# Patch sets of the second block in tiles of their own, and lookups, scatters and weight preparation at other places, in a two-layer codebook convolution

## The chip, the cores and the metric

The kernel runs on one core of one Trainium2 chip. The metric is the device time of one execution in microseconds (us), as the median of several executions. A core has TensorE (PE, matrix products), VectorE (DVE), ScalarE (ACT), GpSimd (POOL) and SyncE (SP), which here only issues transfers; the transfers themselves are moved by 16 DMA engines.

## The reference

The input x is 16 images of 256 channels of 28 x 28. It is normalised in groups of 8 channels, goes through two layers of an approximate 3 x 3 convolution, each with a batch normalisation, and through a squeeze-and-excite gate; the result is added to the normalised and to the raw input.

```python
def amm_conv3x3(x, centroids, w_sub, stride=1):
    patches = jax.lax.conv_general_dilated_patches(x, (3, 3), (stride, stride), 'SAME')
    p = patches.reshape(B, C, s, Ho * Wo).transpose(0, 3, 1, 2)
    d = jnp.sum(p * p, axis=-1)[..., None] - 2.0 * jnp.einsum('bncs,cks->bnck', p, centroids) + jnp.sum(centroids * centroids, axis=-1)[None, None]
    attn = jax.nn.softmax(-d, axis=-1)
    lut = jnp.einsum('cks,cso->cko', centroids, w_sub)
    out = jnp.einsum('bnck,cko->bno', attn, lut)

out = amm_conv3x3(x, centroids1, wsub1, stride=1)
out = jax.nn.relu(bn_inference(out, ...))
out = amm_conv3x3(out, centroids2, wsub2, stride=1)
out = se_layer(bn_inference(out, ...), se_w1, se_b1, se_w2, se_b2)
return jax.nn.relu(out + x)        # x is the group-normalised input; the caller adds the raw one
```

For each channel a patch of 9 values is compared with 16 centroids, and the softmax over them weights the rows of a product of centroids and weights.

## The kernel before

**Blocks and steps.** The work of an image in a layer is cut into four blocks: a half of the channels (`hh`) by a half of the rows (`t`), in the order (0,0), (0,1), (1,1), (1,0). There are 128 blocks, layer 1 first. A block starts every two steps: block j has g = 2j, an image takes 8 steps, layer 2 starts at step 128. The order of all work is written out by hand: `at(step, sub, f, ...)` (L896) files a job under a step and a place within it, and L1111 calls them sorted by that pair. Each call appends its instructions to the queues of the engines it uses, and every engine works through its own queue in that order; an instruction that waits holds up what stands behind it on its engine. TensorE's logits lie at sub 0.1 and 1.1, block sums and numerators (`num_b`, `num_a`) at 1.0, products with the weights at 2.0.

**A block.** `patches(u, p)` (L368) issues six transfers on SyncE that gather the 3 x 3 patches of 64 channels from a padded copy in DRAM (`home1` for layer 1, `home2` for layer 2) into a tile of 128 x 8 x 420. A block has two such sets, p = 0 and 1. There are two tiles, `pts[0]` and `pts[1]`, which all blocks share, so set p of a block is issued at step g + p - 2, after the logits of the block before have read the tile. One row in 16 of the tile stays 1.0 (a bias row); it is filled once at the start, `pts[0]` by ScalarE (L1098) and `pts[1]` by POOL (L1102). `logits` (L380) makes 32 small matmuls for each of four quarters `mm`, ScalarE takes exponentials (`exps`), `num_b` sums the weights, VectorE makes the reciprocal (`recip_dve`) and spreads it over the partitions (`spread`), and `scale_a` (VectorE), or `copy_a` and `scale_q` (ScalarE, POOL) scale the numerators.

**Products.** The four blocks of an image are combined with seven weight tiles of 128 x 9 x 128: A11, A12, A22 and S1 to S4, sums and differences of the weights (a Strassen-like scheme, `PRODUCTS`, L43). POOL makes differences of the activations (`mix`, L527). In layer 1 A11, S3, A22 and A12 are loaded (`load_w`, L194) and S1, S3, S2, S4 are made from them in steps 5 to 8 (`combine`, L207); layer 2 loads all seven near step 128.

**The start.** x of image 0 is loaded in two halves of channels; each is normalised (`norm0`: VectorE, TensorE, POOL, ScalarE) and written to `home1` (`to_home1`, L362). Block 0 and block 1 use the first half of the channels, block 2 and block 3 the second. `center_wd` prepares the centroids (`center_sq` on VectorE, a matmul in `center_add`, then `center_mean`: a reduction, a small multiply and a subtraction, L294). `load_x(1)`, the statistics of image 1 (`gn_stats`) and the loads of A11, S3, A22, A12 follow at steps 1 to 6.

**Preparation during layer 1.** Layer 2 uses its channels in a sorted order that depends on image 0's output. `rank_look` (L664) looks up tables with two indirect transfers of POOL, `rank_cols` copies seven columns for each half; `to_home2` (L593) scatters an image's output with indirect transfers of POOL. Image 0's output is kept in DRAM and read again by `h0_load` and scattered by `h0_put`. The second layer's centroids and weights are laid out in a staging tile `st`: `prep_wd0` to `prep_wd4` centre them in steps 57 to 78 (`prep_wd4`, L739: the mean by VectorE, two subtractions on POOL), `prep_cwa` (L756) makes four multiplies on VectorE and a transfer in step 82, `prep_cwb` (L764) six small POOL operations a part in steps 83, 84, 91 and 92.

The places that matter before:

```python
at(g + p - NPT, 1.5, patches, u, p)                          # L927, NPT = 2
at(*((g - 2, 2.6) if b else (1, 1.65)), load_x, b + 1)        # L1000
at(18, 2.15, rank_look, o)                                    # L1044
at(78, 1.9, prep_wd4)                                         # L1064
at(82, 1.9, prep_cwa)                                         # L1067
at(-0.5, 0.7, to_home1, 0, 1)                                 # L1106
```

Of the kernel before, what the change touches and what calls it, by code (L numbers as in the profile page):

```python
# [8 lines left out]
F32 = mybir.dt.float32  # L9
I32 = mybir.dt.int32  # L10
U32 = mybir.dt.uint32
AF = mybir.ActivationFunctionType
ALU = mybir.AluOpType
# [63 lines left out]
def kernel(  # L77
# [113 lines left out]

    wl = {n: wpool.tile([P, NS, P], F32, name=f"w_{n}") for n in SLOTS}

# [48 lines left out]

    pts = [const.tile([P, 8, PTW], F32, name=f"pt{i}") for i in range(NPT)]
    hpads = [io.tile([P, NPAD], F32, tag="pc", name="hpad", bufs=4) for _ in range(NB)]
    xpads = [io.tile([P, NPAD], F32, tag="pc", name="xpad", bufs=4) for _ in range(NB)]
# [47 lines left out]

    def center_mean(wf, n, eng=None):  # L294
        g = wf.rearrange("p (g k) -> p g k", k=K)
        nc.vector.tensor_reduce(cst[:, : n // K], g, axis=AX.X, op=ALU.add)
        nc.vector.tensor_scalar_mul(cst[:, : n // K], cst[:, : n // K], 1.0 / K)
        (eng or nc.vector).tensor_sub(g, g, cst[:, : n // K].unsqueeze(2).to_broadcast([P, n // K, K]))

# [436 lines left out]
    def prep_wd3(part, step):  # L736
        center_add(pw["st"][:, 512:1536], 384 * part, min(384, 1024 - 384 * part), pw["sq"], step)

    def prep_wd4():  # L739
        st = pw["st"]  # L740
        center_mean(st[:, 512:1536], 1024, nc.gpsimd)
        f = st[:, 512:1536].rearrange("p (g n) -> p g n", n=32)
        nc.gpsimd.tensor_sub(f, f, kbias.unsqueeze(1).to_broadcast([P, 32, 32]))
# [152 lines left out]
    def at(cl, sub, f, *a, **kw):  # L896
        jobs.setdefault((cl, sub), []).append((f, a, kw))
# [23 lines left out]
    for j, u in enumerate(blocks):  # L921
# [3 lines left out]
        for p in range(2):  # L925
            u["pt", p] = pts[p]
            at(g + p - NPT, 1.5, patches, u, p)  # L927
            for q in range(2):
                mm = 2 * p + q
                at(g + p, 0.1 + q, logits, u, mm)  # L930
                if wide and mm == 0:
                    at(g, 0.12, wide_copy, u, mm)
                    at(g, 0.9, wide_turn, u, mm)
                    at(g, 1.38, wide_max, u, mm)
                    at(g, 1.39, wide_sub, u, mm)
                    at(g + 1, 1.22, wide_back, u, mm)
                    at(g + 1, 1.89, wide_exp, u, mm)
                else:
                    at(g + p, 0.12 + q, exps, u, mm)
# [18 lines left out]
    for l in range(2):  # L958
        for b in range(B):
# [30 lines left out]
            if l == 0:  # L990
# [8 lines left out]
                if b + 1 < B:  # L999
                    at(*((g - 2, 2.6) if b else (1, 1.65)), load_x, b + 1)  # L1000
                    for q in range(NB):
# [26 lines left out]

    at(1, 1.66, load_w, 0, "A11")
    at(3, 1.65, load_w, 0, "S3")  # L1030
# [10 lines left out]
    for o in range(2):  # L1041
        at(14, 2.95, rank_make, o)
        at(16, 0.2, rank_sum, o)
        at(18, 2.15, rank_look, o)  # L1044
    for o in range(2):
        at(19 + o, 2.7, rank_cols, o)
        at(24 + 2 * o, 0.6 + 2 * o, h0_load, o)
        for r in range(2):
            at(25 + 2 * o + r, 0.2 if r else 1.9, h0_put, o, r)
        at(32 + 2 * o, 2.6, codes_load, o)  # L1050
# [9 lines left out]
    for part in range(3):  # L1060
        c = (68, 70, 76)[part]
        at(c, 1.95, prep_wd2, part)
        at(c + 1, 2.1, prep_wd3, part, c + 1)
    at(78, 1.9, prep_wd4)  # L1064
    at(78, 2.7, prep_keep, d_wd[1])
    at(80, 2.6, prep_cw0)
    at(82, 1.9, prep_cwa)  # L1067
    for part in range(4):
        at((83, 84, 91, 92)[part], (2.3, 1.5, 2.3, 1.5)[part], prep_cwb, part)
    at(92, 2.7, prep_keep, d_cwb)  # L1070
# [29 lines left out]
    for i in range(2):  # L1100
        to_home1(0, 0, i)
    nc.gpsimd.memset(pts[1], 1.0)  # L1102
    center_wd(0)
    norm0(1)
# [167 lines left out]
```

## Time and profile before

| | us |
|---|---|
| median of 3 runs | 2643.18 (2643.03 to 2647.02) |
| the profiled execution | 2635.26 |
| its span | 2633.8 |
| VectorE busy in it | 1757.6 |
| ScalarE busy | 1357.3 |
| POOL busy | 1898.4 |

The profile is one execution as the hardware profiler saw it, in us from the start of its span. In a timeline row stand the start, the length, the engine, the line of the kernel, the operation, what it writes and reads, the size, and a count where several were merged; in brackets the time for which the engine was idle before it and what ended that. PEld is TensorE's loading of weights, SPq the issue of transfers by SyncE. The chain of waits follows the work that ended last back through what released each piece.

### The profile page before, as it was taken

The page shows a single profiled execution, that of the slowest core. Times are in us where ns is not written, and L with a number is a line of the kernel's source. Part 1 is how long each engine was busy: PE and PEld are TensorE (multiplying, and loading weights), DVE is VectorE, ACT ScalarE, POOL GpSimd, SP SyncE. Part 2 cuts the span into 40 slices and gives each one's busy share as a digit, 9 for nine tenths or more (in the row PEclk, how much of TensorE's full clock was granted, in tenths as well). Part 3 has the DMA queues.
Part 4 walks back from the last instruction along what each step waited for, and adds up shares of the span by engine and source line. Part 5 has one row for each costly group of instructions (what it writes and reads, how often), then busy time and mean ns, then how long its engine had stood idle before and what let it go on. Part 6 is the DMA issues. An engine that isn't in the chain of part 4 may idle for free.

```text
span 2633.8 us, 85661 instructions
## 1 busy us (share of the span) xinstructions
PE 2582.8 (98%) x36984; PEld 1262.6 (48%) x36984; DVE 1757.6 (67%) x3760; ACT 1357.3 (52%) x1874; POOL 1898.4 (72%) x1318
## 2 busy tenths in 40 slices
PE   5999999999999999999999999999999999999997
PEld 2444454444544444544444444444444444444444
DVE  4776566666566665656666776767776667767665
ACT  4444444445444444444455555555555655555653
POOL 2866667766667766687667778778878787777786
PEclk8999999999999999999999999999999999999999
DMA  7656655665455666655664444444444444444441
GB/s 206 163 156 178 192 157 162 189 182 165 141 149 145 173 179 170 174 154 157 163 174 103 115 115 118 129 114 114 106 128 127 117 119 112 116 118 126 114 121 46
DMA packets 217831, 374.37 MB, mean 142 GB/s; under 512 B 29752, under 2 KB 188008, under 8 KB 217448
## 3 DMA queue, kind: packets, MB, share of 16 engines
q1 hardware_dynamic: 211272, 336.16, 48.1%
q0 software_dynamic: 6176, 32.66, 3.4%
q8 instruction: 295, 4.83, 0.8%
q14 instruction: 88, 0.72, 0.1%
HBM read 288.93 MB, written 79.80 MB: 140 GB/s over the span
## 4 chain that ended last, share of the span: by engine, by line
PE 96%; DVE 2%; POOL 1%; DMA 0%; issue 0%; SPq 0%; ACT 0%; DVEq 0%; POOLq 0%; ACTq 0%
PE acc L522 52%; PE lg L388 17%; PE nb L452 14%; PE na L438 13%; DVE rb L495 0%; POOL qp L531 0%; DMA pt<-home 0%; DVE r L480 0%; DVE qp L514 0%; SPq L375 0%; PE sep L820 0%; PE sqp L291 0%; POOL qp L503 0%; PE sep L809 0%; DMA xt<-in_x 0%
## 5 line engine op out<-in xcount | busy, mean ns | idle before, releaser
L399 ACT ACTIVATE e<-lg 128x784 f32<-128x784 f32 x960 | 738.0, 821 | 654.7 <-PE lg L388 652.0
L531 POOL TENSOR_TENSOR qp<-qp,qp 128x784 f32<-128x784 f32 x512 | 943.9, 1868 | 155.1 <-DVE qp L514 154.6
L522 PE MATMUL acc<-qp,w_S 128*128 128x392 f32 x2048 | 733.1, 501 | 2.0 <-POOL qp L531 1.1
L495 DVE STREAM_SHUFFLE rb<-r 128x392 f32<-128x392 f32 x1024 | 550.7, 603 | 0.0
L522 PE MATMUL acc<-qp,w_A 128*128 128x392 f32 x1536 | 546.5, 499 | 0.0
L522 PEld LDWEIGHTS acc<-qp,w_S 128*128 128x128 f32 x2048 | 375.6, 190 | 345.2 <-issue 52.5
L388 PE MATMUL lg<-pt,wd 32*32 32x392 f32 x16384 | 485.4, 502 | 19.8 <-DMA pt<-home 11.1
L522 PEld LDWEIGHTS acc<-qp,w_A 128*128 128x128 f32 x1536 | 284.1, 190 | 247.6 <-DVE qp L514 40.2
L466 DVE SCALAR_TENSOR_TENSOR r<-nb,kst,r 128x392 f32<-128x392 f32 x128 | 79.9, 624 | 467.9 <-ACT r L462 448.3
L452 PE MATMUL nb<-e,cwb 64*32 64x392 f32 x8192 | 375.5, 494 | 0.1
L438 PE MATMUL na<-e,cwa 64*32 64x392 f32 x8192 | 374.4, 492 | 1.1 <-ACT e L399 0.7
L514 DVE TENSOR_TENSOR qp<-na,rb 128x784 f32<-128x784 f32 x352 | 333.4, 971 | 57.8 <-PE na L438 46.9
L503 POOL TENSOR_TENSOR qo<-qo,rb 128x392 f32<-128x392 f32 x128 | 131.3, 1026 | 325.0 <-DVE rb L491 324.4
L480 DVE RECIPROCAL r<-r 128x392 f32<-128x392 f32 x128 | 333.2, 2603 | 4.4
L503 POOL TENSOR_TENSOR qp<-qp,rb 128x784 f32<-128x784 f32 x160 | 297.2, 1868 | 2.9
L452 PEld LDWEIGHTS nb<-e,cwb 64*32 64x32 f32 x8192 | 190.6, 107 | 177.3 <-issue 21.1
L438 PEld LDWEIGHTS na<-e,cwa 64*32 64x32 f32 x8192 | 182.3, 106 | 184.3 <-issue 73.3
L388 PEld LDWEIGHTS lg<-pt,wd 32*32 32x32 f32 x16384 | 120.6, 103 | 295.7 <-issue 247.3
L462 ACT ACTIVATE r<-nb,kst 128x392 f32<-128x392 f32 x128 | 86.8, 678 | 164.9 <-PE nb L452 164.9
L423 POOL TENSOR_TENSOR z<-z,mx 128x1568 f32<-128x1568 f32 x32 | 91.8, 2869 | 94.5 <-DVE mx L417 94.5
L508 ACT COPY qp<-na 128x784 f32<-128x784 f32 x160 | 130.0, 813 | 24.5 <-PE na L438 23.0
L529 POOL TENSOR_TENSOR qo<-qo,qo 128x392 f32<-128x392 f32 x128 | 131.3, 1026 | 0.0
(150 smaller groups left out, 1651.4 us busy)
## 6 DMA issues: line engine op xcount, KB each, us to landing
pt<-home SPq DMA_DIRECT2D x768, 209.0 KB
pt<-home SPq DMA_DIRECT2D x768, 104.5 KB
home<-xpad SPq DMA_DIRECT2D x31, 899.0 KB
xt<-in_x SPq DMA_DIRECT2D x30, 784.0 KB
out_dram<-y SPq DMA_DIRECT2D x32, 392.0 KB
d_wS<-st SPq DMA_DIRECT2D x12, 192.0 KB
w_S<-d_wS SPq DMA_DIRECT2D x4, 576.0 KB
w_A<-in_ws SPq DMA_DIRECT2D x3, 576.0 KB
```

The source lines that it names most:

```text
L388: nc.tensor.matmul(bk[32 * c : 32 * c + 32, :N].rearrange("p (r w) -> p r w", w=W), lhsT=wts["wd", u["hh"]][32 * i : 32 * i + 32, mm, c, : ...
L399: nc.scalar.activation(eg[:, 2 * i : 2 * i + 2, :], bk[:, :, :N], AF.Exp, scale=2.0)
L438: nc.tensor.matmul(bs[32 * i : 32 * i + 32, r, :N], lhsT=wts["cwa", u["hh"]][64 * r : 64 * r + 64, mm, i, :], rhs=es[64 * r : 64 * r + 64, ...
L452: nc.tensor.matmul(bs[32 * i : 32 * i + 32, r, :N], lhsT=wts["cwb", u["hh"]][64 * r : 64 * r + 64, mm, i, :], rhs=es[64 * r : 64 * r + 64, ...
L480: nc.vector.reciprocal(u["r"], u["r"])
L495: nc.vector.stream_shuffle(rb[:, r, :], u["r"], mask_of(2 * mm + r))
L503: nc.gpsimd.tensor_tensor(q, q, u.pop(("rb", mm)), ALU.mult)
L508: nc.scalar.copy(pair(u, mm), u.pop(("na", mm))[:, :, :N])
L514: nc.vector.tensor_mul(pair(u, mm), u.pop(("na", mm))[:, :, :N], rb)
L522: nc.tensor.matmul(accs[key][:, :N], lhsT=wl[w][:, k, :], rhs=us["q", k], start=first and n == 0, stop=last and n == len(ks) - 1,)
L529: nc.gpsimd.tensor_tensor(out_u["q", 8], in0["q", 8], in1["q", 8], ALU.subtract)
L531: nc.gpsimd.tensor_tensor(pair(out_u, mm), pair(in0, mm), pair(in1, mm), ALU.subtract)
```

## The change

- The six weight tiles other than A11 become slices of two tiles: `walls[0]` holds S1, S2, S4 and `walls[1]` holds A12, S3, A22. `alts[0]` and `alts[1]` are views of the first 3360 columns of each, in the shape of a patch tile. Block 1 alone takes its patches into `alts`, whose columns hold no weights until step 3. Their bias rows are filled at the start, `alts[0]` by POOL after `pts[1]`, `alts[1]` by ScalarE.
- Block 1's two sets are issued at (-0.9, 0.0) and (-0.4, 0.0), on either side of the transfer of x's second half to `home1` (-0.5, 0.7). Block 2's sets go to (0, 1.5) and (1, 1.5), two steps earlier. `load_x(1)` and `load_w(A11)` move from step 1 to step 0, behind block 2's first set.
- `rank_look` moves from step 18 to 17, `rank_cols` for both halves to step 18; `h0_load` of the second half and three of the four `h0_put` move one to three steps later.
- `center_mean` is split: `center_sum` makes the mean. The late centring makes its mean at (77, 2.2) and its two POOL subtractions at (78, 0.5) instead of all at (78, 1.9).
- `prep_cwa` moves from step 82 to 83, the first part of `prep_cwb` from (83, 2.3) to (84, 0.5).

```diff
-    wl = {n: wpool.tile([P, NS, P], F32, name=f"w_{n}") for n in SLOTS}
+    walls = [wpool.tile([P, 3, NS, P], F32, name=f"wall{i}") for i in range(NPT)]
+    wl = {n: walls[i // 3][:, i % 3] for i, n in enumerate(("S1", "S2", "S4", "A12", "S3", "A22"))}
+    wl["A11"] = wpool.tile([P, NS, P], F32, name="w_A11")
...
+    alts = [
+        w.rearrange("p a s n -> p (a s n)")[:, : 8 * PTW].rearrange("p (s n) -> p s n", n=PTW) for w in walls
+    ]
...
-    def center_mean(wf, n, eng=None):
+    def center_sum(wf, n):
+        nc.vector.tensor_reduce(cst[:, : n // K], wf.rearrange("p (g k) -> p g k", k=K), axis=AX.X, op=ALU.add)
+        nc.vector.tensor_scalar_mul(cst[:, : n // K], cst[:, : n // K], 1.0 / K)
+
+    def center_mean(wf, n):
+        center_sum(wf, n)
         g = wf.rearrange("p (g k) -> p g k", k=K)
-        nc.vector.tensor_reduce(cst[:, : n // K], g, axis=AX.X, op=ALU.add)
-        nc.vector.tensor_scalar_mul(cst[:, : n // K], cst[:, : n // K], 1.0 / K)
-        (eng or nc.vector).tensor_sub(g, g, cst[:, : n // K].unsqueeze(2).to_broadcast([P, n // K, K]))
+        nc.vector.tensor_sub(g, g, cst[:, : n // K].unsqueeze(2).to_broadcast([P, n // K, K]))
...
+    def prep_wd_sum():
+        center_sum(pw["st"][:, 512:1536], 1024)
+
     def prep_wd4():
         st = pw["st"]
-        center_mean(st[:, 512:1536], 1024, nc.gpsimd)
+        g = st[:, 512:1536].rearrange("p (g k) -> p g k", k=K)
+        nc.gpsimd.tensor_sub(g, g, cst.unsqueeze(2).to_broadcast([P, 64, K]))
         f = st[:, 512:1536].rearrange("p (g n) -> p g n", n=32)
         nc.gpsimd.tensor_sub(f, f, kbias.unsqueeze(1).to_broadcast([P, 32, 32]))
...
-            u["pt", p] = pts[p]
-            at(g + p - NPT, 1.5, patches, u, p)
+            u["pt", p] = alts[p] if j == 1 else pts[p]
+            if j == 1:
+                at(-0.4 if p else -0.9, 0.0, patches, u, p)
+            else:
+                at(g + p - (2 * NPT if j == 2 else NPT), 1.5, patches, u, p)
...
-                    at(*((g - 2, 2.6) if b else (1, 1.65)), load_x, b + 1)
+                    at(*((g - 2, 2.6) if b else (0, 1.65)), load_x, b + 1)
...
-    at(1, 1.66, load_w, 0, "A11")
+    at(0, 1.66, load_w, 0, "A11")
...
-        at(18, 2.15, rank_look, o)
+        at(17, 1.9, rank_look, o)
     for o in range(2):
-        at(19 + o, 2.7, rank_cols, o)
-        at(24 + 2 * o, 0.6 + 2 * o, h0_load, o)
+        at(18, 2.7, rank_cols, o)
+        at(24 + 4 * o, 0.1 if o else 0.6, h0_load, o)
         for r in range(2):
-            at(25 + 2 * o + r, 0.2 if r else 1.9, h0_put, o, r)
+            at(*((25, 1.9), (27, 1.9), (28, 1.96), (30, 1.85))[2 * o + r], h0_put, o, r)
...
-    at(78, 1.9, prep_wd4)
+    at(77, 2.2, prep_wd_sum)
+    at(78, 0.5, prep_wd4)
...
-    at(82, 1.9, prep_cwa)
+    at(83, 1.9, prep_cwa)
     for part in range(4):
-        at((83, 84, 91, 92)[part], (2.3, 1.5, 2.3, 1.5)[part], prep_cwb, part)
+        at((84, 84, 91, 92)[part], (0.5, 1.5, 2.3, 1.5)[part], prep_cwb, part)
...
     nc.gpsimd.memset(pts[1], 1.0)
+    nc.gpsimd.memset(alts[0], 1.0)
+    nc.scalar.activation(alts[1].rearrange("p s n -> p (s n)"), one.to_broadcast([P, 8 * PTW]), AF.Copy)
```

## The prediction

> **What bounds the kernel now.** I read the page first (engines), then the busy time by 80 us windows, then the chain of work that ended last, then the timelines of the stretches where TensorE is not busy.
>
> ```profile
> PE 2582.8 (98%) x36984; PEld 1262.6 (48%) x36984; DVE 1757.6 (67%) x3760; ACT 1357.3 (52%) x1874; POOL 1898.4 (72%) x1318
> ```
> ```profile
> 0.00:80.00 80.00, 46.69 (x807) 19.27 (x808) 38.44 (x99) 33.35 (x41) 26.80 (x42) 0.91 0.80 216
> ...
> 800.00:880.00 80.00, 76.61 (x1092) 36.87 (x1077) 53.84 (x124) 36.33 (x50) 56.00 (x50) 1.00 0.60 155
> ```
>
> The busy line of the page gives PE 2582.8 us of a span of 2633.8 us: 51.0 us idle. In the windows (each engine's busy us, instructions in brackets, then granted clock, DMA share, GB/s), the first one holds 80.00 - 46.69 = 33.3 us of it and 800:880 another 3.4 us. Most of the rest is the drain at the end, which the change does not touch. So TensorE sets the time, and an edit can gain only by closing one of these gaps, or lose by opening a new one.
>
> The chain of waits (start, length, what) shows how the steady part beats. The same product of consecutive images starts at:
>
> ```profile
> 791.32 6.12 PE acc L522 x18
> ...
> 876.11 6.12 PE acc L522 x18
> ...
> 956.13 6.12 PE acc L522 x18
> ```
>
> 876.11 to 956.13 is the undisturbed period, 80.02 us. 791.32 to 876.11 is 84.79, so 4.77 us too long. That is image 9, where the second layer's weights are prepared. Steps below count ten-microsecond job slots; this stretch is steps 77 to 85.
>
> The first 70 us are the fill. TensorE's timeline (bracket: idle before, and what ended it):
>
> ```profile
> 19.16 1.22 PE L291 MATMUL sqp<-sq,nhalf_sb 128*128 128x256 f32 x2 [0.85 <-DVE sq L286]
> 22.99 3.30 PE L388 MATMUL lg<-pt,wd 32*32 32x392 f32 x64 [2.61 <-DMA pt<-home]
> 28.41 2.39 PE L388 MATMUL lg<-pt,wd 32*32 32x392 f32 x64 [2.12 <-DMA pt<-home]
> 37.21 1.62 PE L388 MATMUL lg<-pt,wd 32*32 32x392 f32 x32 [6.40 <-DMA pt<-home]
> ...
> 61.59 0.95 PE L388 MATMUL lg<-pt,wd 32*32 32x392 f32 x32 [1.48 <-ACT e L399]
> ```
>
> The logits of block 0 run at 22.99 and 28.41, end at 28.41 + 2.39 = 30.80, and then TensorE sits 6.40 us until the first patch set of block 1 has landed at 37.1. That is the largest wait in the fill, and the one the change aims at.
>
> **The start: block 1's patches.** Why they are late is in SyncE's queue:
>
> ```profile
> 14.68 7.59 SPq L375 DMA_DIRECT2D pt<-home  x12
> 22.38 0.58 SPq L366 DMA_DIRECT2D home<-xpad  x1
> 26.32 8.59 SPq L375 DMA_DIRECT2D pt<-home  x12
> ```
>
> Twelve patch transfers of block 0 leave from 14.68 to 22.27; then the second half of x goes to home1 (L366); then the queue stands until 26.32, because block 1 is written into the same `pts`, which block 0's logits read until 22.99 + 3.30 = 26.29. Now they go to `alts`, so the first six leave at 22.3 without that wait and ahead of the home1 write; the write follows at about 26, the other six behind it to about 30.
>
> Issuing earlier is not landing earlier. The windows of 5 us and the sizes (KB each, from the list of DMA issues):
>
> ```profile
> 25.00:30.00 5.00, 2.88 (x96) 0.89 (x64) 0.00 (x0) 3.31 (x5) 0.00 (x0) 0.98 0.82 240
> 30.00:35.00 5.00, 0.81 (x20) 0.00 (x0) 0.00 (x0) 2.37 (x4) 0.00 (x0) 0.50 0.90 200
> ```
> ```profile
> pt<-home SPq DMA_DIRECT2D x768, 209.0 KB
> pt<-home SPq DMA_DIRECT2D x768, 104.5 KB
> home<-xpad SPq DMA_DIRECT2D x31, 899.0 KB
> xt<-in_x SPq DMA_DIRECT2D x30, 784.0 KB
> ```
>
> The engines are 0.82 and 0.90 busy at 240 and 200 GB/s while TensorE waits, so this is bandwidth, not only queue order. What the first set of block 1 really gains is that 899 KB no longer go ahead of it: 899 KB at 240 to 200 GB/s are 3.7 to 4.5 us; I take **4.1**. The bounds: 0, if the write is served side by side with the patches and costs them the same bandwidth as before; 6.4, if the set lands before 30.80, where TensorE's own work begins to decide. I stay in the middle because the queue is served roughly in order: block 0's second set, issued by 22.27, let logits start at 28.41 although the write was queued right behind it.
>
> What is late next? After block 1's first logits the fill is a chain of latencies (numerators, reciprocal, spreads, scaling, each freeing a PSUM bank) which slides forward as a whole, if transfers keep up. Per set 3 x 209.0 + 3 x 104.5 = 940.5 KB. With block 1's first set down at 37.1 - 4.1 = 33.0, there follow the write 899, block 1's second set 940.5, block 2's first 940.5 and x(1) 784 KB, since SyncE cannot issue block 2 (its patches read that write) nor x(1) behind it before the write has landed. 3564 KB at 240 to 200 GB/s end at 47.9 to 50.8. x(1) is needed by the statistics:
>
> ```profile
> 54.48 1.02 DVE L319 BATCH_NORM_STATS2 gn_st<-xt 128x6 f32<-128x392 f32 x2
> ...
> 58.97 0.16 DVE L329 COPY gn_gm<-gnp 128x4 f32<-128x4 f32 x1 [2.07 <-PE gnp L325]
> ```
>
> 54.48 - 4.1 = 50.4, and VectorE then has 2.07 us of idle before it is needed again. So x(1), though the queue gives it a later place behind block 2's first set, arrives with 1.7 to 4.6 us to spare, and nothing is charged; if it fails, `gn_stats` holds VectorE's queue (join_r and the reciprocal of block 1 stand behind it), and each us past the cover is a us of TensorE. This also caps the start's gain near 54.48 + 2.07 - 50.8 = 5.8 at the lower rate: beyond that x(1) would be last. Weight loads A11, S3, A22 sit in this queue earlier than before, or at the same place, and their users keep theirs.
>
> The clock adds an error of about one. At 30 to 35 us the granted clock was 0.50; 32 logits took 1.62 us at 37.21 and 0.95 us at 61.59. Moving the idle stretches moves the half-speed stretches too; one such burst more or less is 0.7 us and I put nothing in the sum.
>
> **The two added fills.** ScalarE's (alts[1]) lies in its 7.92 us wait before the second normalisation, more than twice what POOL takes for an equal tile (below), and is free. POOL's is not quite:
>
> ```profile
> 18.41 1.04 ACT L354 ACTIVATE xpad<-xt,nrm 128x784 f32<-128x784 f32 x1 [7.92 <-POOL nrm L348]
> ```
> ```profile
> 9.35 2.89 POOL L1102 MEMSET pt<- 128x3360 f32 x1
> ...
> 20.63 1.64 POOL L1113 MEMSET hpad<- 128x900 f32 x2
> ```
> ```profile
> 12.61 0.18 DVE L297 TENSOR_SCALAR cst<-cst 128x32 f32<-128x32 f32 x1
> ...
> 21.59 0.72 DVE L297 TENSOR_SCALAR cst<-cst 128x32 f32<-128x32 f32 x1
> ```
>
> The fill of `pts[1]` takes POOL 2.89 us, to 12.24; a second one takes it to 15.13, before its next work. But the small multiply L297 took 0.18 us at 12.61, with POOL idle, and 0.72 us at 21.59, ending where POOL's two fills of `hpad` (20.63 to 22.27) end. So at 12.61 it will now be held until 15.13, 2.5 us. Behind it in VectorE's queue stand the second normalisation and centring, whose last matmul in TensorE's queue (19.16 + 1.22 = 20.38) moves to 22.9, ahead of logits that start at 22.99. Cover 2.6 us for 2.5: I charge **0.1**, between 0 and 0.5. The second half of x, now 2.5 us later from ScalarE too, is sent only at 26 and loses nothing.
>
> The Trainium skill, page "SBUF — State Buffer", section "Who interferes with whom", says that a VectorE instruction in a two-port mode and a GpSimd instruction exclude each other for the whole of the one that came first. Row 21.59 agrees. By the rule taken with no exception any of VectorE's one-input operations near the fill could be held, which would make the term no larger than the 2.89 us of one fill less its cover, 0.3, and the sum -7.8.
>
> **The middle: centring and weights of layer 2.** Chain row, then timeline of all engines:
>
> ```profile
> 797.44 0.43 PE sqp L291 x2
> ```
> ```profile
> 802.36 0.63 DVE L466 SCALAR_TENSOR_TENSOR r<-nb,kst,r 128x392 f32<-128x392 f32 x1 [4.03 <-ACT r L462]
> ...
> 808.00 1.20 DVE L296 TENSOR_REDUCE cst<-st 128x64 f32<-128x1024 f32 x1
> ...
> 809.51 1.94 POOL L298 TENSOR_TENSOR st<-st,cst 128x1024 f32<-128x1024 f32 x1 [4.70 <-DVE cst L297]
> ...
> 811.52 2.38 POOL L743 TENSOR_TENSOR st<-st,kst 128x1024 f32<-128x1024 f32 x1
> ...
> 824.34 0.93 PE L522 MATMUL acc<-qo,w_S 128*128 128x392 f32 x2 [1.70 <-POOL qo L529]
> ...
> 826.13 1.58 PE L522 MATMUL acc<-qp,w_S 128*128 128x392 f32 x4 [0.87 <-POOL qp L531]
> ...
> 848.67 2.23 DVE L761 TENSOR_SCALAR st<-st,kst 128x256 f32<-128x256 f32 x4
> ```
> ```profile
> 860.84 0.16 DVE L344 TENSOR_TENSOR gn_var<-gn_gm,gnp 128x2 f32<-128x2 f32 x1 [4.28 <-PE gnp L342]
> ...
> 877.14 1.02 POOL L503 TENSOR_TENSOR qo<-qo,rb 128x392 f32<-128x392 f32 x1 [5.02 <-DVE rb L491]
> ```
>
> Before, the mean's reduction (L296, 1.20 us) runs in step 78 between VectorE's spreads, and POOL, idle for 4.70 us, waits for it and only then subtracts (1.94 + 2.38 us, to 813.9). POOL's next differences are that much late, and TensorE waits 1.70 + 0.87 us for them at 824 and 826. The change puts the reduction after step 77's addition, where VectorE idles 4.03 us before 802.36, and the subtractions at the head of step 78: POOL is free from 809.51 - 4.70 = 804.8, so it is done at 804.8 + 4.3 = 809.1, 4.8 us earlier. The small multiply may be held by one POOL operation (under 2 us by the rows on fills and differences), still inside the 4.03.
>
> The four multiplies for cwa (L761, 2.23 us) likewise stood among step 82's spreads. In step 83 they follow the last spread and precede 860.84, with 4.28 us idle. The first cwb part on POOL slides behind a scatter into step 84; POOL's next wait, 5.02 us before 877.14, takes it up. If that were gone, POOL's scaling would be late by what exceeds it. The write of cwa on SyncE now stands behind step 83's patches, which leave first, so patches gain rather than wait; the write of the centred rows is no longer held by POOL.
>
> Of the 4.77 us, 0.43 is the centring matmul itself, which stays; 4.34 can go. I take **4.0**, leaving 0.3 for residues; bounds 0 (POOL no earlier after all) and 4.3.
>
> **Lookups and scatters.**
>
> ```profile
> 193.42 2.01 POOL L566 TENSOR_TENSOR hpad<-hpad,half_sum 128x392 f32<-128x392 f32 x2 [3.21 <-DVE hpad L559]
> ...
> 203.82 1.11 POOL L666 DMA_INDIRECT idx<-in_ids,ri  x1 [0.17 <-issue]
> ...
> 208.60 1.02 POOL L503 TENSOR_TENSOR qo<-qo,rb 128x392 f32<-128x392 f32 x1 [2.41 <-DVE rb L491]
> ```
>
> The two lookups (1.11 us the first) move ahead of the work at 193.42, into POOL's 3.21 us idle; the fourteen column copies land where the lookups were, before the 2.41 us idle of 208.60. The scatters of image 0 spread out so that they stop splitting differences. The load of the second half of h0 on SyncE now waits for the scatter in step 27 to release its buffer; the patches behind it wait for logits anyway. With POOL idle on both sides of this work I charge 0, between -0.1 and +1 (one scatter's time on POOL in front of a difference).
>
> **Sum.** -4.1 + 0.1 - 4.0 + 0 = -8.0 us. The profiled execution took 2635.26 us around its span of 2633.8; the median of the runs shown is 2643.18, 7.9 above. 2635.26 - 8.0 = 2627.3 in the profile's terms, **2635.2** in the median's.
>
> **Rivals.** (a) More: the set lands by 30.80 (6.4), middle 4.3, and the half-speed stretches shrink by two bursts (1.4): -12.1, 2631.1. For: engines at 0.82 leave room. Against: 0.90 at 200 GB/s, and the x(1) cap.
>
> (b) The start yields nothing: home write and patches share the engines, the set lands near 37 as before, and only the middle counts: 2639.2. For: DMA share near full. Against: the queue order seen at 28.41. Within the bound of no change.
>
> (c) The middle does not do what it says, because POOL's differences queue behind the same two subtractions: -4.0 from the start alone, 2639.2. Against: the 4.70 us idle.
>
> (d) Slower: x(1). SyncE stands before block 2's patches until the home1 write has landed, and x(1) is issued behind both; VectorE then stops at `gn_stats`. Each us after 54.48 - 4.1 + 2.07 = 52.5 costs one. It eats the start's gain at 56.6 and passes the middle's 4.0 at 60.6, from where the kernel is slower; with x(1) at 66 the price is 5.4 net, 2648.6. For: the longest queue in front of one load. Against: it needs 3564 KB to run at under 130 GB/s, and both windows quoted run at 200 or more.
>
> **Chances.** Forecast 0.60 (2632 to 2637.5), (a) 0.13, (b) 0.14, (c) 0.07, (d) 0.06. What a measurement of this kernel can tell from no change is 0.2%, 5.3 us, so below 2637.9 is faster: the forecast, (a) and a little of (b) and (c), 0.76; same 0.18; slower 0.06. The range, 2629.5 to 2640.5, takes in (a), (b) and (c) with an us or so of the clock's error and leaves (d) out; the forecast's own is 2632 to 2637.5.
>
> **What would show it.** Start: SyncE's six first transfers of block 1 at 22.3, the home1 write near 26, first logits of block 1 near 33 (37.1: rival b; 31: rival a). Fill: L297 near 12.6 lasting about 2.6 us, last centring matmul near 22.9. Middle: L298 at about 804.8 less the start's gain, no TensorE wait for POOL after it, and the period there at 80.5. It would be wrong if `gn_stats` of image 1 waits for x(1), or if a product now waits on a weight load into the shared tiles.

## The result, and the profile after

The changed kernel takes 2633.00 us as the median of six executions (2630.99 to 2634.69); the kernel before took 2643.11 in the same comparison (2640.61 to 2647.02). The ratio is 0.9959, 95% interval 0.9948 to 0.9969: 10.1 us less by the medians (which alone give 0.9962; the ratio and its interval are an estimate of their own). The forecast was 2635.2.

The spans of the two profiled executions do not show it: 2633.8 us before, 2633.2 after. The profiled execution of before (2635.26) lies 5.4 us below the fastest of its six timed ones; the profiled one of the changed kernel (2634.69) is the slowest of its six. So single stretches can be compared between the traces, the spans cannot.

The windows of 80 us (busy time of each engine, then granted clock, DMA share, GB/s), after:

```profile
0.00:80.00 80.00, 50.95 (x809) 20.48 (x810) 41.41 (x101) 37.07 (x43) 30.23 (x44) 0.96 0.81 216
800.00:880.00 80.00, 78.69 (x1120) 39.03 (x1115) 59.41 (x124) 37.71 (x51) 58.17 (x51) 1.00 0.60 162
```

In the middle window TensorE is busy 2.08 us more (76.61 before). In the first it is busy 4.26 us more with two matmuls more: part of that is matmuls that took longer (those at 51.50 and 53.82 below, where the granted clock was 0.50 from 50 to 55 us), so busy time alone is no gain here.

**The start.** SyncE's queue, then TensorE's timeline, after:

```profile
22.40 5.23 SPq L383 DMA_DIRECT2D wall<-home  x6
28.68 0.58 SPq L374 DMA_DIRECT2D home<-xpad  x1
29.72 4.48 SPq L383 DMA_DIRECT2D wall<-home  x6
```
```profile
21.47 1.22 PE L296 MATMUL sqp<-sq,nhalf_sb 128*128 128x256 f32 x2 [0.85 <-DVE sq L291]
23.42 3.30 PE L396 MATMUL lg<-pt,wd 32*32 32x392 f32 x64 [0.73 <-DVE wd L297]
29.84 3.30 PE L396 MATMUL lg<-pt,wd 32*32 32x392 f32 x64 [3.12 <-DMA pt<-home]
34.53 1.62 PE L396 MATMUL lg<-wall,wd 32*32 32x392 f32 x32 [1.39 <-DMA wall<-home]
...
51.50 2.39 PE L396 MATMUL lg<-pt,wd 32*32 32x392 f32 x32
53.82 4.18 PE L460 MATMUL nb<-e,cwb 64*32 64x392 f32 x64
...
68.24 4.22 PE L530 MATMUL acc<-qp,w_A 128*128 128x392 f32 x12
```

The first six transfers of block 1 leave at 22.40, where they were forecast (22.3). But they take 5.23 / 6 = 0.87 us each where the twelve before them took 7.59 / 12 = 0.63, and the `home1` write goes out at 28.68 instead of 26. The view of waits (total us, times, longest) for SyncE from 22 to 29 us says where the time went:

```profile
SPq L383 <- DMA pt<-home: 1.6, 4, 0.6
SPq L374 <- DMA pt<-home: 1.0, 1, 1.0
```

By this view issuing itself was not slower, (5.23 - 1.6) / 6 = 0.6 us each: SyncE stood still four times (1.6 us) until one of block 0's transfers had landed, and 1.0 us more before the write. Block 0's second set now shares the engines with block 1's transfers: its logits start at 29.84, 1.43 us later than before (28.41). Block 1's first logits start at 34.53, before at 37.21: 2.7 us gained where 4.1 were forecast, and TensorE's wait there is 1.39 instead of 6.40. By the first product with A11 at 68.24 only 0.6 of it is left, since before has

```profile
68.86 4.22 PE L522 MATMUL acc<-qp,w_A 128*128 128x392 f32 x12
```

**The added fill.** VectorE's and POOL's timelines, after:

```profile
12.59 2.50 DVE L301 TENSOR_SCALAR cst<-cst 128x32 f32<-128x32 f32 x1
...
12.16 2.89 POOL L1119 MEMSET wall<- 128x3360 f32 x1
```

The small multiply is held to the end of POOL's fill (12.16 + 2.89 = 15.05), 2.50 us, as forecast, and the last centring matmul ends at 21.47 + 1.22 = 22.69 (forecast: near 22.9).

**The middle.** The chain of waits, then the timelines of VectorE, POOL and TensorE, after:

```profile
792.51 6.12 PE acc L530 x18
...
874.97 6.12 PE acc L530 x18
```
```profile
799.55 1.22 DVE L300 TENSOR_REDUCE cst<-st 128x64 f32<-128x1024 f32 x1
800.81 5.24 DVE L301 TENSOR_SCALAR cst<-cst 128x64 f32<-128x64 f32 x1
805.97 0.61 DVE L474 SCALAR_TENSOR_TENSOR r<-nb,kst,r 128x392 f32<-128x392 f32 x1
...
797.64 5.55 POOL L539 TENSOR_TENSOR qp<-qp,qp 128x784 f32<-128x784 f32 x3
803.16 1.01 POOL L537 TENSOR_TENSOR qo<-qo,qo 128x392 f32<-128x392 f32 x1
804.13 1.86 POOL L539 TENSOR_TENSOR qp<-qp,qp 128x784 f32<-128x784 f32 x1
806.12 1.93 POOL L753 TENSOR_TENSOR st<-st,cst 128x1024 f32<-128x1024 f32 x1
...
809.77 0.95 PE L396 MATMUL lg<-pt,wd 32*32 32x392 f32 x32 [1.31 <-issue]
```

and the same multiply in the timeline of before, where POOL was idle:

```profile
809.23 0.20 DVE L297 TENSOR_SCALAR cst<-cst 128x64 f32<-128x64 f32 x1
```

The disturbed period is 874.97 - 792.51 = 82.46 us; it was 84.79, and 80.5 were forecast. The reduction stands where it was put, and TensorE's waits for POOL at 824 and 826 are gone. But the multiply L301 (128 x 64 numbers) takes 5.24 us instead of 0.20: it starts under the second of POOL's five operations in a row (differences, three of them in the first line) and ends when the fifth ends (804.13 + 1.86 = 805.99). POOL's next operation, at 806.12, is the one that needs the mean (`cst`), so the train ended there. VectorE's join for the reciprocal (L474) comes 5.2 us after the reduction, and TensorE's next logits wait 1.31.

### The profile page after: what moved, and what is told of

Its sections match the earlier page's. It is cut to its first block, busy times and chain, and to the rows that moved or that the text cites. A ratio compares the mean times of both kernels' runs of the same rounds, so it can differ in the third digit from the quotient of the medians.

```text
span 2633.2 us, 85671 instructions
## 1 busy us (share of the span) xinstructions
PE 2587.9 (98%) x36984; PEld 1266.7 (48%) x36984; DVE 1767.3 (67%) x3760; ACT 1360.2 (52%) x1875; POOL 1900.5 (72%) x1319
## 4 chain that ended last, share of the span: by engine, by line
PE 97%; DVE 1%; DMA 1%; POOL 0%; issue 0%; ACT 0%; SPq 0%; DVEq 0%; POOLq 0%; ACTq 0%
PE acc L530 52%; PE lg L396 17%; PE nb L460 14%; PE na L446 14%; DMA wall<-home 0%; DMA pt<-home 0%; DVE rb L503 0%; SPq L383 0%; DVE qp L522 0%; DVE r L488 0%; PE sep L832 0%; DMA home<-xpad 0%; POOL qp L539 0%; PE sep L821 0%; DMA xt<-in_x 0%
## 5 line engine op out<-in xcount | busy, mean ns | idle before, releaser
L530 PE MATMUL acc<-qp,wall 128*128 128x392 f32 x3072 | 1096.7, 500 | 1.8 <-DVE rb L499 1.0
L530 PEld LDWEIGHTS acc<-qp,wall 128*128 128x128 f32 x3072 | 565.2, 190 | 509.2 <-issue 55.0
L474 DVE SCALAR_TENSOR_TENSOR r<-nb,kst,r 128x392 f32<-128x392 f32 x128 | 80.1, 626 | 460.2 <-ACT r L470 444.5
L530 PE MATMUL acc<-qp,w_A 128*128 128x392 f32 x512 | 182.3, 499 | 0.0
L530 PE MATMUL acc<-qo,wall 128*128 128x392 f32 x384 | 157.7, 492 | 0.0
L516 ACT COPY qp<-na 128x784 f32<-128x784 f32 x160 | 130.0, 812 | 23.8 <-PE na L446 22.3
L530 PEld LDWEIGHTS acc<-qp,w_A 128*128 128x128 f32 x512 | 94.6, 190 | 82.8 <-DVE qp L522 20.4
```

What stands on the lines that cost most here:

```text
L516: nc.scalar.copy(pair(u, mm), u.pop(("na", mm))[:, :, :N])
L530: nc.tensor.matmul(accs[key][:, :N], lhsT=wl[w][:, k, :], rhs=us["q", k], start=first and n == 0, stop=last and n == len(ks) - 1,)
```

## The experiments

Ratios stand against executions of the kernel before beside them on the same chip. The runs were made on three chips: r1 to r4 on the first (median of the kernel before 2638.99), r5 to r8 on the second (2643.38), r9 to r12 on the third (2643.20). Which chip the first two profiles came from is not on record.

### The spread of one profile, and the parts alone

First the kernel before again and the changed kernel again, both without an edit, beside two kernels with one part each.

> The kernel before, unchanged, for a second profile and for the spread of its times. Theory A (the first profile is typical, and what it lost at the start and in the middle is what the change could win): its profile again loses about 4.3 us in steps 78 to 83 and its product of step 5 starts near 68.9 us. Theory B (the first profile was a lucky execution, since it is 5 to 12 us below every timed run): the time is 2640 to 2647 and the trace shows 5 us or more of TensorE idle that the first one does not have; where it lies says what the change really removed.

Measured: 2639.0, ratio 1.0002 [0.9993, 1.0011], its profiled span 2637.1. The first theory holds in the main: the middle loses the same again (4.79 us over the undisturbed period), though the span is 3.3 us longer.

> The changed kernel, unchanged, for a second profile. If start and middle are all, its ratio is the product of the two parts (0.997 under A); under B it stays at 0.996, and its profile against that of the kernel before of the same call differs by about 10 us, not by 0.6 as the first pair.

Measured: 2632.53, 0.9974 [0.9963, 0.9985], 6.5 us less, span 2628.4. The two intervals of the same kernel, 0.9959 and 0.9974, just overlap.

It is the kernel before that differs, not the changed one: the changed kernel took 2633.00 in the first comparison and 2632.53 here, the kernel before 2643.11 and 2638.99, and 2643.38 and 2643.20 on the two other chips. So some 4 of the 10.1 us are a cost that the kernel before has on some chips and not on the first. (Each chip was used on one occasion only, so chip and occasion cannot be told apart.) The profiled execution of before (2635.26) fits the first chip, where the kernel before took 2634.23 to 2642.48; it is shorter than every execution of it on the two others.

The changed kernel thus had spans of 2633.2 and 2628.4. By the first product with A11 2.8 of the 4.8 us are there, and matmuls at half clock are the largest piece of that. Windows of 5 us of the first trace of the changed kernel, then of the second, with the second's timeline of TensorE:

```profile
50.00:55.00 5.00, 4.86 (x80) 0.92 (x60) 4.97 (x13) 3.21 (x4) 2.85 (x2) 0.50 0.87 237
```
```profile
50.00:55.00 5.00, 4.21 (x109) 1.82 (x116) 4.43 (x13) 3.40 (x5) 2.92 (x2) 1.00 1.00 227
```
```profile
50.72 1.06 PE L396 MATMUL lg<-pt,wd 32*32 32x392 f32 x32 [0.81 <-DVE qp L522]
51.71 2.86 PE L460 MATMUL nb<-e,cwb 64*32 64x392 f32 x64
...
58.47 1.62 PE L396 MATMUL lg<-pt,wd 32*32 32x392 f32 x32 [2.28 <-DMA pt<-home]
...
65.43 0.93 PE L530 MATMUL acc<-qp,w_A 128*128 128x392 f32 x2
```

At a granted clock of 0.50 logits and block sums of block 2 took 2.39 and 4.18 us, at 1.00 they took 1.06 and 2.86: 2.65 us for the same 96 matmuls; the first products lie 2.81 apart (68.24 and 65.43). Where the clock is full, another wait shows: 2.28 us for block 2's second set at 58.47, which the forecast did not name.

So the start is better read over many traces. The first product with A11 starts at (us):

| block 1's start | first product with A11 |
|---|---|
| as before (before, r1, r3, r8, r10) | 68.86, 70.39, 69.24, 71.37, 70.51: mean 70.07 |
| as changed (after, r2, r4, r5, r6, r9, r11) | 68.24, 69.42, 65.43, 64.25, 65.78, 69.44, 65.06: mean 66.80 |

The start is worth 3.3 us by these means, with a spread of 5 among the changed ones. The same traces have block 1's first logits 2.7 us earlier in the mean (34.69 against 37.37), and block 0's second logits later without exception: 29.76 to 30.12 in the seven, 28.41 to 28.69 in the five.

The part at the start alone (own tiles, order, fills; the middle and the lookups as before):

```diff
-            at(g + p - NPT, 1.5, patches, u, p)
+            if j == 1: at(-0.4 if p else -0.9, 0.0, patches, u, p)
...
-                    at(*((g - 2, 2.6) if b else (1, 1.65)), load_x, b + 1)
+                    at(*((g - 2, 2.6) if b else (0, 1.65)), load_x, b + 1)
```

> Of the change only the start: block 1's sets in alts, their bias fills, the order of the queue, x(1) and A11 one step earlier. Theory A: about half of the gain, ratio 0.998 (4 to 5 us). Theory B with the excess in the start: nearly the whole 10 us, ratio 0.996; with the excess elsewhere: 0 to 1 us, as the two profiles show it at step 5 (68.9 against 68.2).

Measured: 2636.76, 0.9992 [0.9982, 1.0001], span 2635.1: 2.2 us less by the medians, with an interval that just takes in no change. Its trace has the fill's gain at block 1 (first logits at 35.72) and gives it back at block 2's second set, for which TensorE waits 4.75 us at 62.30.

The middle alone:

```diff
-    at(78, 1.9, prep_wd4)
+    at(77, 2.2, prep_wd_sum)
+    at(78, 0.5, prep_wd4)
...
-    at(82, 1.9, prep_cwa)
+    at(83, 1.9, prep_cwa)
```

> Of the change only the middle: the mean at (77, 2.2), the subtractions at (78, 0.5), cwa in step 83, cwb at (84, 0.5). By the two profiles the middle gains 2.3 us and not 4.0 (4.28 us of excess in steps 78 to 83 before, 2.01 in 78 and 79 after): ratio 0.999. As predicted it would be 4.0, ratio 0.9985. Step 78 should again show the small multiply of the mean lasting about 5 us.

Measured: 2635.24, 0.9988 [0.9979, 0.9997], span 2631.7. The excess in steps 77 to 86 (intervals between groups of 32 logits, less their median over undisturbed images) falls from 4.77 us to 2.05; in the first trace of the whole change it falls to 2.45. The small multiply takes 5.24 us here too.

The lookups and scatters alone, twice, and the whole change without them:

```diff
-        at(18, 2.15, rank_look, o)
+        at(17, 1.9, rank_look, o)
...
-        at(19 + o, 2.7, rank_cols, o)
+        at(18, 2.7, rank_cols, o)
...
-            at(25 + 2 * o + r, 0.2 if r else 1.9, h0_put, o, r)
+            at(*((25, 1.9), (27, 1.9), (28, 1.96), (30, 1.85))[2 * o + r], h0_put, o, r)
```

> Of the change only the lookups and scatters, on the kernel before. As predicted: 0, between -0.1 and +1 us; steps 17 to 31 keep their 80.02 us period, the 0.12 us of excess at step 19 may move to step 18. If the three parts add up, this is the rest between the sum of start (0.9992) and middle (0.9988) and the whole (0.9974): at most 1.5 us.

> The same kernel as in the run with the lookups alone (before, with only the lookups, the column copies, the load of h0 and its scatters moved), once more, beside other runs of before. Theory 1 (spread): a ratio whose interval reaches 1, about 0.9995 to 1.0005. Theory 2 (the move is worth 3 us): 0.9988 again. The trace should show the fill and the middle as before (first logits of block 1 near 37, 3 us or more lost in step 80).

> The changed kernel with the lookups, the column copies, the load of h0 and its scatters at their old places. Alone, the move of these took 0.12% off (0.9988 [0.9979, 0.9997]), and no trace shows where. Theory 1 (the 0.12% is the spread between executions, since the trace of the lookups alone shows no shorter step between 17 and 31): 0.9960 to 0.9972 of before, the same as the changed kernel's 0.9959 and 0.9974, and steps 17 to 31 as long as in the changed kernel within 0.3 us. Theory 2 (the move is worth 3 us): 0.9975 to 0.9985, and a wait of TensorE of some us in steps 17 to 31 that the changed kernel does not have.

Measured: alone 2639.53, 0.9988 [0.9979, 0.9997], and again 2639.73, 0.9987 [0.9978, 0.9996]; the whole without them 2637.53, 0.9974 [0.9965, 0.9983]. The last lies between its two theories, but both intervals of the lookups alone leave out 1, so the theory that this is only spread between executions falls: on these two chips the part that was charged nothing is worth about 0.12%, 3 us, as much as either other part.

Four traces with the old places do not show it; the fifth, of the whole without the lookups' move, does. Its timelines of TensorE's weight loads (numerators of step 19) and of POOL:

```profile
204.31 0.20 PEld L446 LDWEIGHTS na<-e,cwa 64*32 64x32 f32 x13 [0.64 <-issue]
204.91 0.17 PEld L446 LDWEIGHTS na<-e,cwa 64*32 64x32 f32 x4 [0.40 <-issue]
205.65 0.17 PEld L446 LDWEIGHTS na<-e,cwa 64*32 64x32 f32 x5 [0.58 <-issue]
206.38 0.15 PEld L446 LDWEIGHTS na<-e,cwa 64*32 64x32 f32 x5 [0.56 <-issue]
...
204.40 1.11 POOL L674 DMA_INDIRECT idx<-in_ids,ri  x1 [0.15 <-issue]
205.81 0.97 POOL L674 DMA_INDIRECT idx<-in_ids,ri  x1 [0.30 <-issue]
```

and the weight loads at the same place in the timeline of before:

```profile
203.73 1.01 PEld L438 LDWEIGHTS na<-e,cwa 64*32 64x32 f32 x32 [0.64 <-issue]
```

Before, 32 loads go out in 1.01 us. Here they come four or five at a time with gaps of 0.40 to 0.58 us, "issue": TensorE waited for nothing that the profile shows, while POOL's two lookups ran (204.40 to 206.78). The numerators took 5.00 us instead of 3.04. The same pattern returns in the logits at 301.16, beside a scatter of h0 (301.00, 0.97 us), 2.20 us instead of 0.94. Over steps 19 to 28 that trace's excess is 4.4 us. None of the nine traces with the new places has more than 0.2 us in any of steps 17 to 31, but neither have the other four with the old ones.

The same pattern stands elsewhere too, in step 79, where numerators run beside a scatter. POOL and the weight loads in the first trace of the changed kernel:

```profile
810.64 0.98 POOL L602 DMA_INDIRECT home<-hpad,col  x1 [0.15 <-issue]
...
810.65 0.20 PEld L446 LDWEIGHTS na<-e,cwa 64*32 64x32 f32 x15 [0.64 <-issue]
811.21 0.24 PEld L446 LDWEIGHTS na<-e,cwa 64*32 64x32 f32 x3 [0.36 <-issue]
811.90 1.57 PEld L446 LDWEIGHTS na<-e,cwa 64*32 64x32 f32 x46 [0.46 <-issue]
```

These numerators took 3.54 us; in the second trace of the changed kernel, beside the same scatter, they took 2.96 without such a gap. What goes with the pattern is the chip. An execution has 76 indirect transfers. Beside them none of the four traces from the first chip has a gap of more than 0.28 us between these small weight loads once the fill is over; of the eight traces from the two other chips seven have, and the whole without the lookups' move most (nine gaps, 4.3 us). Those are the chips on which the kernel before takes some 4 us more.

So it is shown that the move gains some 3 us on these two chips, and that indirect transfers can go with a stall of TensorE's issue. That the kernel before pays the stall there in every timed execution fits all these numbers but is not shown, since no trace of that kernel is known to come from those chips; why the chips differ is open. Nor does every such stall stand beside an indirect transfer: the run with x(1) behind block 2's second set (below) has one of 2.35 us at 91.9, beside POOL's differences.

The parts were not all measured on one chip, so they cannot simply be added. On the first chip start and middle make 0.8 + 1.2 = 2.0 thousandths of the whole's 2.6, which leaves 0.6 (1.6 us) for the lookups, with about 1 either way on each figure; on the two others the lookups alone make 1.2 and 1.3.

### The middle: what holds the multiply

```diff
-        center_sum(pw["st"][:, 512:1536], 1024)
+        nc.vector.tensor_reduce(cst, wf.rearrange("p (g k) -> p g k", k=K), axis=AX.X, op=ALU.add)
+        nc.scalar.mul(cst, cst, 1.0 / K)
```

> The changed kernel with one instruction moved: the small multiply of the late mean (64 columns) runs on ScalarE instead of VectorE. Theory 1 (the middle lost 2 us of its gain because that multiply, 5.24 us instead of 0.20, was held on VectorE until POOL's queue of differences ran dry): TensorE's excess in steps 77 to 86 falls from 2.05-2.45 us to about 0.45, the centring matmul alone, and the kernel is 1.5 to 2 us faster than the changed one (ratio to before 0.9966 where that had 0.9974). Theory 2 (it is the subtractions on POOL, early or not, that hold up step 78): no change there.

Measured: 2631.13, 0.9955 [0.9942, 0.9969]: 1.7 us under the next run, which has the changed kernel's time, with intervals that overlap, so the gain is read in the trace. With the multiply on ScalarE, the timelines of ScalarE, VectorE and POOL, then the chain of waits:

```profile
796.22 0.26 ACT L750 ACTIVATE cst<-cst 128x64 f32<-128x64 f32 x1 [6.65 <-DVE cst L749]
...
798.96 0.63 DVE L474 SCALAR_TENSOR_TENSOR r<-nb,kst,r 128x392 f32<-128x392 f32 x1 [2.77 <-ACT r L470]
...
793.06 5.53 POOL L539 TENSOR_TENSOR qp<-qp,qp 128x784 f32<-128x784 f32 x3
```
```profile
787.92 6.12 PE acc L530 x18
...
868.88 6.12 PE acc L530 x18
```

0.26 us instead of 5.24, under the same train of POOL's operations; VectorE then has 2.77 us to spare before L474, and the period is 868.88 - 787.92 = 80.96 us, 1.5 less than with the multiply on VectorE. That leaves 0.94 over the undisturbed 80.02, where 0.45 was expected. The forecast's 80.5 was nearly right for the schedule and wrong for the engine of one small operation.

### The start: what order, tiles, fill and late loads are worth

A11 back behind block 2's second set, then `load_x(1)` and A11 both back:

```diff
-    at(0, 1.66, load_w, 0, "A11")
+    at(1, 1.66, load_w, 0, "A11")
```

> The changed kernel with the load of A11 (576 KB) back at step 1, behind block 2's second patch set. Theory 1 (that second set, not x(1), is what came late next: TensorE waited 2.28 us for it at 58.5 in one run of the changed kernel and 4.75 us at 62.3 in the start alone): the wait in step 5 goes, the first logits of step 5 start near 56 and the product of step 5 near 63; 0 to 2.5 us faster than the changed kernel. Theory 2 (step 5 is set by the chain of reciprocals and scalings): no change, 60 to 61.

Measured: 2632.83, 0.9962 [0.9948, 0.9975], the same as the changed kernel. SyncE's queue and TensorE's timeline with A11 behind that set:

```profile
43.22 4.91 SPq L383 DMA_DIRECT2D pt<-home  x6
...
58.48 1.62 PE L396 MATMUL lg<-pt,wd 32*32 32x392 f32 x32 [2.26 <-DMA pt<-home]
```

The six transfers leave right behind x(1), and the logits that need them start at 58.48, against 58.47 with A11 ahead of them (the second trace of the changed kernel): no gain from the place of A11's 576 KB is seen. Up to 0.9 us of one could hide, since x(1) left 0.9 us later in this trace (42.15 against 41.27).

```diff
-                    at(*((g - 2, 2.6) if b else (0, 1.65)), load_x, b + 1)
+                    at(*((g - 2, 2.6) if b else (1, 1.65)), load_x, b + 1)
...
-    at(0, 1.66, load_w, 0, "A11")
+    at(1, 1.66, load_w, 0, "A11")
```

> The changed kernel with both x(1) and A11 at step 1, behind block 2's second set, as in the kernel before. Rival (d) of the prediction in its own place: VectorE's statistics of image 1, due near 52, now wait for x(1), which lands 4 to 6 us later, near 54 to 56; TensorE's small matmul behind block 1's sums waits 1 to 3 us, and what block 2's second set gains is given back. If x(1) has slack instead, this is as fast as the run with A11 alone moved or faster.

Measured: 2635.82, 0.9971 [0.9962, 0.998], 3.0 us above the run before by the medians (eleven executions from 2633.98 to 2640.08, five from 2630.66 to 2634.12). This is the prediction's slower rival, brought about by the order of the queue. SyncE issues x(1) at 48.32 (42.15 in the run before), and by the timelines VectorE and then TensorE wait for it:

```profile
56.26 1.04 DVE L327 BATCH_NORM_STATS2 gn_st<-xt 128x6 f32<-128x392 f32 x2 [3.26 <-DMA xt<-in_x]
...
58.83 0.45 PE L333 MATMUL gnp<-gn_mv,gmat 128*128 128x4 f32 x2 [3.47 <-DVE gn_mv L328]
```

In the run before, the statistics waited 0.47 us, and the first product with A11 stands at 65.78 there against 70.10 here. So `load_x(1)` at step 0 is what keeps the rival away.

Both sets of block 1 in their own tiles, but behind the `home1` write:

```diff
-                at(-0.4 if p else -0.9, 0.0, patches, u, p)
+                at(-0.35 if p else -0.4, 0.0, patches, u, p)
```

> The changed kernel with both sets of block 1 in their own tiles, but issued behind the write of x's second half to home1 instead of on either side of it. It tells whether the fill gains by the tiles (no wait for the logits that read the old ones) or by the order (940 KB ahead of 899 KB). Theory 1 (order and bandwidth, as the prediction has it): the first logits of block 1 start at 36.5 to 37.2 as in before instead of 34.5, block 2's first set, which needs that write, lands 2 to 3 us earlier than in the changed kernel, and the time is that of the changed kernel within 1 us since the fill's end is set by block 2's sets: 0.996 to 0.997. Rival (the tiles): first logits of block 1 at 34.5 or before, since the queue no longer stands until 26.3, and the time is 0 to 2 us under the changed kernel's.

Measured: 2634.26, 0.9965 [0.9951, 0.9978]. SyncE's queue and TensorE's timeline:

```profile
22.43 0.58 SPq L374 DMA_DIRECT2D home<-xpad  x1
23.44 12.96 SPq L383 DMA_DIRECT2D wall<-home  x12
...
38.76 1.62 PE L396 MATMUL lg<-wall,wd 32*32 32x392 f32 x32 [5.50 <-DMA wall<-home]
```

The queue no longer stands until 26.3, and yet the first logits come at 38.76, later than before (37.21) and than either theory had it. The rival (the tiles) falls: what block 1's first logits gain, they gain by the 940 KB that go ahead of the 899 KB. The other half of theory 1 falls too: block 2's first set leaves no earlier (37.40 against 36.54 in the changed kernel), and its first logits come at 55.65 against 50.72 in the second trace of the changed kernel, part of it at half clock. Block 0's second logits start at 29.95 here, as late as in the changed kernel, so the transfers that delay them need not stand right behind them in the queue. What the order is worth in time this run does not tell: its first product with A11 stands at 72.36, 5.6 us behind the mean of the changed start, but that is its slowest execution (2637.48), and its median is the changed kernel's within the intervals.

Last, the multiply on ScalarE as above and the first fill on ScalarE too:

```diff
-    nc.gpsimd.memset(alts[0], 1.0)
+    nc.scalar.activation(alts[0].rearrange("p s n -> p (s n)"), one.to_broadcast([P, 8 * PTW]), AF.Copy)
```

> The changed kernel with two operations taken off the pair VectorE and POOL: the small multiply of the late mean on ScalarE (alone it gave 0.9955 of before), and the fill of block 1's first tile by ScalarE instead of POOL. Theory 1 (the multiply at 12.6 is held for the whole of POOL's fill and nothing else holds it): that multiply takes 0.2 us instead of 2.50, the last centring matmul ends 2.2 to 2.4 us earlier, at 20.3 to 20.5, and the first logits start when their patches have landed, 0.2 to 0.5 us earlier than the 23.42 of the changed kernel; no more, since the patches set the rest. Time 0.0 to 0.5 us under the kernel with the mean alone: 2626 to 2631, 0.9950 to 0.9956. Rival (the fill costs nothing): the first logits stay at 23.4. Rival 2 (ScalarE's two fills, 6 us, delay its normalisation of x's second half): that activation, 20.71 in the changed kernel, does not come earlier, and the write of x's second half follows later than 28.7.

Measured: 2631.07, 0.9953 [0.9939, 0.9967]. VectorE's and TensorE's timelines:

```profile
12.52 0.18 DVE L301 TENSOR_SCALAR cst<-cst 128x32 f32<-128x32 f32 x1
...
19.07 1.22 PE L296 MATMUL sqp<-sq,nhalf_sb 128*128 128x256 f32 x2 [0.85 <-DVE sq L291]
23.56 3.30 PE L396 MATMUL lg<-pt,wd 32*32 32x392 f32 x64 [3.27 <-DVE bnsc L279]
```

The hold is gone (0.18 us), the centring ends 2.4 us earlier at 20.29, and the first logits start at 23.56, no earlier than 23.42. The rival holds: in this trace POOL's fill costs nothing. Rival 2 falls: ScalarE normalises x's second half at 18.32 instead of 20.71. Yet the write of it goes out at 28.71, as in the changed kernel, since SyncE stands before it with block 1's first set. The kernel is the same as with the mean alone; both are some 12 us (0.45%) under before and have the lowest medians measured here.

## Why the prediction was right, and where it was not

The time, 2633.0, lies 2.2 us from the forecast and inside its own range. The sum was -8.0; measured were -10.1, and -6.5 the second time. But the terms that make it are not the forecast's: two were put too high and one at nothing, and it is partly luck that they made up for each other.

- **Start, -4.0 net.** The queue moved as described, and for block 1's first logits the cause is the one named: order, not tiles. Sized too large at block 1 (2.7 us instead of 4.1): the step that failed is "the queue is served roughly in order". Block 0's second set lost 1.43 us to the transfers behind it, and the write left 2.7 us later than put. At the first product the mean over traces is 3.3; the start alone took 2.2 us off, with an interval that just takes in no change.
- **What is late next.** x(1) was named as the cap. Where the place of `load_x(1)` was the changed kernel's it was late by 0.47 us at most; block 2's second set was later (2.28 us at 58.47). With x(1) left at its old place the slower rival's wait did come and cost 3.0 us, with the kernel still under before.
- **The added fill, 0.1.** The hold came as put (2.50 us), and without it nothing was gained. (By its own cover, 2.6 us for 2.5, the term is 0; the 0.1 is a margin.) The Trainium skill, page "SBUF — State Buffer", section "Who interferes with whom", has a VectorE instruction in a two-port mode and a GpSimd instruction exclude each other for the whole of the one that came first; that agrees with the 2.50 us at this place.
- **Middle, -4.0.** The order was right, the period fell by 2.33. (A fall of 4.0 would have left 80.8; the 80.5 under "What would show it" takes all of the 4.34 off.) The step that failed is "The small multiply may be held by one POOL operation (under 2 us by the rows on fills and differences)": it was held past three boundaries between POOL's operations, 5.24 us, and the 4.03 us of idle did not cover it. The same train stands in the trace of before, from 796.45 to 804.81, over the whole of that idle stretch (798.33 to 802.36), and could have been read there. With the multiply on ScalarE the period fell by 3.83, nearly what was put. The Trainium skill's sentence on the pair, in the same section, speaks of one instruction and does not reach this far; the measurement decides.
- **Lookups and scatters, 0.** This step failed by the most on two chips: some 3 us gained, below the bound of -0.1. It was read from one trace in which TensorE lost 0.12 us there. On the first chip, whose traces show no more, start and middle leave it 1.6 us or nothing.
- **From profile to median, 7.9 us held constant.** It was 7.9 for before (2643.11 - 2635.26) and -1.7 for the changed kernel (2633.00 - 2634.69). The sum held for the medians, not for the profiled executions on which it was made. Some 4 of the 7.9 is what the kernel before differs by between chips, if the first trace is from a chip like the first; the changed kernel does not show this difference.
- **Clock.** One burst more or less was put at 0.7 us and left out. Between two traces of one kernel it made 2.65.

The weight loads into the shared tiles held no product, and the rivals fell: (a) block 1's set did not land by 30.80; (b) its logits came at 34.5, not 37; (c) TensorE no longer waited for POOL after the late subtraction.

## What to carry to other kernels

Where a profiled execution lies outside the timed ones, its span is no base for a sum: compare stretches, and a stretch that ends in a fill over several traces. A change of 0.3% is to be timed on more than one chip: here the kernel before differed by 4 us between chips and the changed one by 0.5. Look also whether the trace shows what the timed executions pay. A small VectorE operation that POOL can hold is to be charged the whole train of POOL operations it falls into (here up to the first gap), not one of them; ScalarE took the same multiply in 0.26 us. A transfer issued earlier is paid for by the one that is on the way already.

## What the hardware showed that was not expected

- A multiply of 128 x 64 on VectorE took 5.24 us instead of 0.20 under POOL operations that followed each other without a gap; it did not get in between two of them.
- TensorE's small weight loads came with gaps of up to 0.58 us while POOL issued indirect transfers, with no releaser in the profile: in none of four traces from one chip, in seven of eight from two others.
- SyncE's six patch transfers took 0.87 us each while block 0's sets were under way, and 0.63 before: four times it waited until an earlier transfer had landed.
- The half-speed stretches of TensorE's clock fell at 50 to 55 us in one trace of the changed kernel and not in the other, 2.65 us apart on the same matmuls.
